# Two-layer convolution block on one core: the tail of layer 0 is rewritten so that its tiles keep pixels on partitions

## The chip, the cores and the metric

The kernel runs on one core of one Trainium2 chip. The metric is the device time of one execution in microseconds. A core has a matrix engine (TensorE, PE in the profile, its weight loads as PEld), a vector engine (VectorE, DVE), an activation engine (ScalarE, ACT), GpSimd (POOL) and SyncE (SP), which only issues DMAs here. Each engine runs its own instructions strictly in the order in which the program lists them; semaphores make one engine wait for another.

## The reference

The input `x` has shape (2, 256, 128, 128): two images of 256 channels. Two residual layers follow each other, each behind a group norm:

```python
x = x + L0(gn(x))          # three deformable branches, a 1x1 convolution and an MLP
x = x + conv3x3(gn(x), ternary(weight)) + bias
# L0, for xg = gn(x):
x_i = gelu(ln2d(deform_dw(xg, conv3x3(xg, off_w_i)), bw_i, bb_i))   # i = 1, 2, 3; dilations 1, 9, 12
c   = conv_w @ xg + conv_b                                          # 1x1
out = ln2d(x_1 + x_2 + x_3 + c, n1_w, n1_b)
h   = gelu(out @ mlp_w1.T + mlp_b1) @ mlp_w2.T + mlp_b2             # per pixel, 256 -> 512 -> 256
out = ln2d(h + out, n2_w, n2_b)
```

`ln2d` normalises each pixel over its 256 channels and then applies a weight and a bias per channel. The inputs set `bw_i`, `n1_w`, `n2_w` to ones and `bb_i`, `n1_b`, `n2_b` to zeros.

## The kernel before, in words

The program has three stages. Stage A normalises `x`, writes it pixel by pixel to a table in DRAM, computes the offsets of the three branches and from them bilinear weights ("hats"), which also go to DRAM. The middle stage samples the table, and runs the rest of layer 0 (the "tail") beside the sampling. Stage C is the second layer's convolution. A flag computed between stage A and the middle stage (`beyond`) chooses between the fast sampling (`sample_near`) and a general path (`sample_any`); the inputs here take the fast one.

**Sampling.** A unit is (image, block of two image rows, branch). For each unit the vector engine builds a matrix `A` by multiplying hats (`build`, L1088, three instructions for the three rows of taps), into one of two `A` buffers. Then come two passes, one for each half of the channels (`sample`). In a pass the matrix engine multiplies 11 tiles of the table by `A` into PSUM tiles `pm` (L1173; an fp32 matmul shows as two records, so 22 records a pass); ACT copies each pair of tiles from PSUM to a tile `ev` (L1182); the vector engine accumulates from `ev` into a ring of image rows, one `SCALAR_TENSOR_TENSOR` for each tap (`accumulate`, L1150). There are four `pm` banks and three `ev` tiles. `A` for unit u+2 is built by the vector engine ahead of the accumulation of the second pass of unit u: it can be built only when the matrix engine is done with unit u, and the matrix engine can't start unit u+2 before it is built.

**A cycle.** Four image rows (512 pixels, a "group") take two row blocks of three branches, so six units or twelve passes. These are called pass 0 to pass 11 below: 0 and 1 are the first branch of the even row block, 2 and 3 the second, 4 and 5 the third, 6 to 11 the same for the odd row block. There are 64 groups.

**The tail.** When the rows of a group are complete in a branch's ring, a generator `Tail.branch` is begun. It runs in steps beside the sampling: `sample` calls `tail.advance()` before and in the middle of each pass's matmuls, and each step issues its instructions there. A `yield n` lets n advances go by; a second number says how many big tiles the branch holds from then on, which `may` weighs against `VBUFS` (9 tiles) and `PEAK`. All instructions on PE, ACT and DVE in this stage are pinned to the order in which Python issues them (`pin`). For one branch of a group the tail does:

- `normalised`: eight 128x128 transposes on PE (L824) turn the ring's rows so that pixels lie on partitions, with a correction by bf16 matmuls (L832); two ACT copies bring them to a tile `T` (L840); four `bn_stats` and four `bn_aggr` on DVE give mean and variance of every pixel (L848, L850); four small POOL instructions give scale and bias (L852 to L855); after five advances, four ACT instructions normalise `T` in place (L859); eight more transposes (L871) turn it back to channels on partitions, into two PSUM tiles `zc`;
- two ACT instructions apply GELU with `bw` and `bb` from PSUM (L887); the result is added to the earlier branches' through DRAM (`g12d`; L901, L931);
- after the third branch, `finish` adds the 1x1 product of `x` minus its mean (L802 `pc`, L927 on DVE), normalises the sum (`normalised`, then L937), does both products of the MLP (L802 `hp` and `h`, GELU L950, sum L965), normalises again (`normalised`), applies `n2_w`, `n2_b` and `x` (L980, L986), takes statistics for layer 1 (L990) and stores.

So `normalised` runs five times for each group, with 16 transposes each time.

Of the kernel before, what the change touches and what calls it, by code (L numbers as in the profile page):

```python
# [19 lines left out]
P = 128  # L20
W = 128
C = 256
KC = C // P
HID = 512
MC = HID // P
R = 4
NG = R * W
# [7 lines left out]
LN_EPS = 1e-6  # L35
# [15 lines left out]
BRS = (0, 1, 2)  # L51
NORMS = 3
VBUFS = 9
PEAK = 3
GAP = 2
LAG = 5
XCLS = (0, 1, 3, 9, 11)
# [14 lines left out]
def conv_preact_kernel(ctx: ExitStack, tc: tile.TileContext, t: dict, out: bass.AP):  # L72
    nc = tc.nc
    x = t["x"]
    NB, _, H, _ = x.shape
# [13 lines left out]
    nc.vector.tensor_copy(ident_b, ident)  # L89
    mhalf = const.tile([P, NG // P], F32, name="mhalf")  # L90
    nc.vector.memset(mhalf, -0.5)

    later = []

# [5 lines left out]
    def load_now():  # L100
# [50 lines left out]
    x1d = dram("x1d", [C, HW])  # L151
# [306 lines left out]
    with ExitStack() as actx:  # L458
        psum = actx.enter_context(tc.tile_pool(name="ps_a", bufs=1, space=PSUM))

        def gps():
            return psum.tile([P, 512], F32, name="gnps", tag="tp", bufs=2)

        ap = actx.enter_context(tc.tile_pool(name="apool", bufs=1))
        dxs = sorted({d * s for d in DILS for s in (-1, 0, 1)})
        k = {
            "dxs": dxs,
            "zero": ap.tile([P, C], F32, name="zero"),
            "wz": ap.tile([P, KC, NZ], F32, name="wz"),
            "shift": ap.tile([P, len(dxs), P], F32, name="shift"),  # L470
            "mid": ap.tile([P, ZG, NOFF], F32, name="mid"),
            "hatw": ap.tile([P, 2, NTAP * NH], BF16, name="hatw"),
            "parts": [ap.tile([P, 2, ZG, P], BF16, name=f"parts{i}") for i in range(2)],
            "zr": ap.tile([P, ZRING, NZ], F32, name="zr"),
            "planes": [ap.tile([P, 2, NG], BF16, name=f"planes{i}") for i in range(2)],
        }
        nc.vector.memset(k["zero"], 0.0)
        for parts in k["parts"]:
            nc.vector.memset(parts, 0.0)
        XT = min(4, NGRP)  # L480
        beside = store_signs(ap)
        for b in range(NB):
            stats = ap.tile([P, KC, NGRP, 6], F32, name=f"stats1_{b}", tag=f"stats1_{b}")
            for c in range(KC):
                for g0 in range(0, NGRP, XT):
                    xt = ap.tile([P, XT * NG], F32, name="xt", tag="xt", bufs=3)
                    nc.sync.dma_start(
                        xt,
                        x[b, c * P : (c + 1) * P].rearrange("p h w -> p (h w)")[
                            :, g0 * NG : (g0 + XT) * NG  # L490
                        ],
                    )
                    for j in range(XT):
                        nc.vector.bn_stats(stats[:, c, g0 + j, :], xt[:, j * NG : (j + 1) * NG])
            if b == 0:
                load_now()
                nc.sync.dma_start(k["wz"], t["wz"].rearrange("(k p) n -> p k n", p=P))
                nc.sync.dma_start(k["shift"], t["shift"])
                nc.sync.dma_start(k["mid"], t["mid"])
                hatw = ap.tile([P, 2, NTAP * NH], F32, name="hatw32", tag="xt", bufs=3)  # L500
                nc.sync.dma_start(hatw, t["hatw"])
                nc.vector.tensor_copy(k["hatw"], hatw)
                pattern = ap.tile([P, NG], F32, name="pattern", tag="xt", bufs=3)
                nc.sync.dma_start(pattern[HALF : HALF + NPAT], t["pattern"])
# [12 lines left out]
            phase_a(b, ap, psum, k, beside)  # L517
        for _ in beside:
            pass
# [218 lines left out]
    with tc.tile_pool(name="mpool", bufs=1) as mpool:  # L738
        with tc.tile_pool(name="ps_m", bufs=1, space=PSUM) as ps_m:
            miss = missing(ps_m, mpool)  # L740
        ids = miss["ids"]
        farall = small.tile([P, 1], F32, name="farall", tag="farall")
        nc.gpsimd.partition_all_reduce(farall, miss["worst"], P, bass.bass_isa.ReduceOp.max)
        flag = const.tile([P, 1], I32, name="flag")
        nc.vector.tensor_scalar(flag, farall, 0.0, None, ALU.is_gt)
        beyond = nc.values_load(flag[0:1, 0:1], min_val=0, max_val=1)
# [6 lines left out]
    class Tail:  # L753
# [48 lines left out]
                    nc.tensor.matmul(out, lhsT=w, rhs=v, start=i == 0, stop=i == n - 1)  # L802
                )

        def normalised(self, z, src, what=None):

            pool, pin = self.pool, self.pin
            NB4 = NG // P  # L810
            while self.norms == NORMS:
                yield 1
            self.norms += 1
            T = self.tile("T")
            Tv = T.rearrange("p k n -> p (k n)").rearrange("p (j c) -> p j c", c=C)
            S = self.spots.get(what and what[0::2])
            tps = [self.bank("tp") for h in range(NB4 // 2)]
            for h in range(NB4 // 2):
# [19 lines left out]
            for h in range(NB4 // 2):  # L838
                pin(
                    nc.scalar.copy(  # L840
                        Tv[:, 2 * h : 2 * h + 2, :].rearrange("p j c -> p (j c)"), tps[h]
                    )
                )
            self.read.add(what)
            st = pool.tile([P, NB4, 6], F32, name="st", tag="st", bufs=NORMS)
            mv = pool.tile([P, NB4, 2], F32, name="mv", tag="mv", bufs=NORMS)
# [147 lines left out]
            )  # L994


    def sample_near(pool, psum, k):

        pin = tc.keep_in_program_order
        count = pool.tile([P, NG], F32, name="count")  # L1000
        nc.sync.dma_start(count, t["count"].partition_broadcast(P))
        tail = Tail(pool, psum, pin)
        units = [(b, Rt, br) for b in range(NB) for Rt in range(NR) for br in BRS]
        xts, hbs, owners, begun = {}, {}, {}, set()
        done = {(b, br): 0 for b in range(NB) for br in BRS}
# [618 lines left out]
```

## Time and profile before

| | |
|---|---|
| runs shown | 7072.38, 7077.51, 7089.49 us; median 7077.51 |
| the profiled execution | 7086.97 us; span of its instructions 7085.2 us |
| stage A | from the start to 975 us, when the first hats are loaded back |
| middle stage, first to last sampling matmul | 983.6 to 5896.0 us |
| rest of the tails, without sampling | 5896 to 6035 us |
| stage C | from 6046 us on |

The page lists for each engine its busy time; a view by windows gives the same for any stretch of the span; the view of groups gives, for each line and shape, count, busy time and mean duration. Records of matmuls overlap: a record of PE lasts some 0.16 us longer than the time until the next one starts. What an instruction costs its engine is therefore read from the start of one run of equal instructions to the start of what follows it, in the timeline. The timeline merges equal instructions (`x8`) and shows in brackets how long the engine sat idle before them and what ended that.

### The profile page before, as it was taken

To read this page: it belongs to the slowest core of one execution; us is meant where nothing else is said; L and a number is where in the kernel's file an instruction comes from. 1 tells how busy PE (TensorE), PEld (TensorE's weight loads), DVE (VectorE), ACT (ScalarE), POOL (GpSimd) and SP (SyncE) were. 2 spreads that over 40 slices of the span, in tenths; PEclk is the share of its full clock that TensorE was granted. 3 is DMA by queue.
4 is the path that set the end of the run, shared out by engine and by line. 5 is a ranking of instruction groups with operands and counts; after the bars stand their busy time and mean duration, and the time that the engine had idled before them with its cause. 6 is when DMAs were issued, how large, how long until landed. Compare 5 with 4: busy or idle time off the path is not lost. (4 is left out here: it accounts for less than half of the span.)

```text
span 7085.2 us, 104557 instructions
## 1 busy us (share of the span) xinstructions
PE 6716.0 (95%) x33906; PEld 5091.4 (72%) x33906; DVE 5861.9 (83%) x13016; ACT 4654.2 (66%) x9398; POOL 811.4 (11%) x1307
## 2 busy tenths in 40 slices
PE   6899969999999999999999999999999999899999
PEld 3455558888888888888788888888888885344444
DVE  7766658999989999998689899989989985875775
ACT  2344437788878878877777788788878876332332
POOL 0000010111111111111111111111111111000000
PEclk9999979999999999999999999999999999999999
DMA  8876657777777777776667777777777762221211
GB/s 289 254 205 185 189 152 219 221 215 210 213 213 213 217 212 217 211 209 202 179 195 219 208 218 213 213 213 213 216 208 216 217 203 86 100 81 69 75 70 51
DMA packets 671955, 1330.29 MB, mean 188 GB/s; under 512 B 109736, under 2 KB 290008, under 8 KB 667168
## 3 DMA queue, kind: packets, MB, share of 16 engines
q1 hardware_dynamic: 653408, 1288.49, 61.3%
q10 hardware_dynamic: 17408, 33.56, 1.5%
q8 instruction: 273, 4.47, 0.3%
q14 instruction: 290, 2.38, 0.1%
q0 software_dynamic: 576, 1.39, 0.1%
HBM read 1057.07 MB, written 266.08 MB: 187 GB/s over the span
## 5 line engine op out<-in xcount | busy, mean ns | idle before, releaser
L1173 PE MATMUL pm<-A,xs 96*128 96x216 f32 (+2 forms) x17424 | 3267.5, 342 | 132.3 <-ACT ev L1182 81.3
L1173 PEld LDWEIGHTS pm<-A,xs 96*128 96x128 f32 x17424 | 3055.0, 193 | 367.7 <-issue 152.8
L1150 DVE SCALAR_TENSOR_TENSOR ring<-ev,defw,ring 128x256 f32<-128x256 f32 (+4 forms) x6372 | 2482.9, 451 | 160.1 <-ACT ev L1182 100.3
L1182 ACT COPY ev<-pm 128x432 f32<-128x432 f32 (+2 forms) x4752 | 2032.5, 475 | 708.2 <-PE pm L1173 592.6
L1088 DVE TENSOR_TENSOR A<-hy,hx 96x768 f32<-96x768 f32 (+1 forms) x1124 | 1005.2, 943 | 287.1 <-PE pm L1173 235.8
L1458 PE MATMUL pc<-cring,signs 128*128 128x512 bf16 x4608 | 1007.6, 382 | 20.0 <-ACT cring L1405 13.3
L1458 PEld LDWEIGHTS <-signs 128*128 128x128 bf16 x4608 | 452.4, 98 | 574.5 <-issue 30.1
L859 ACT ACTIVATE T<-T,rs 128x256 f32<-128x256 f32 x1280 | 663.2, 592 | 20.8 <-POOL rs L855 20.7
L852 POOL TENSOR_SCALAR rs<-mv 128x4 f32<-128x4 f32 x320 | 123.2, 385 | 4205.2 <-DVE mv L850 2905.1
L802 PE MATMUL hp<-T,w 128*128 128x512 f32 x1024 | 482.9, 595 | 2.5 <-ACT T L937 2.5
L329 PE MATMUL pz<-wz,xa 128*128 128x486 f32 x1024 | 467.0, 585 | 16.7 <-DVE zr L336 16.7
L848 DVE BATCH_NORM_STATS2 st<-T 128x6 f32<-128x256 f32 x1280 | 446.7, 410 | 30.3 <-ACT T L840 30.3
L802 PE MATMUL h<-hT,w 128*128 128x512 f32 x1024 | 460.5, 592 | 0.0
L1132 ACT ACTIVATE ring<-ev,defw 128x256 f32<-128x256 f32 (+1 forms) x856 | 404.5, 485 | 24.1
L1466 ACT ACTIVATE o<-xl,l1b 128x1024 f32<-128x1024 f32 x64 | 73.5, 1148 | 500.9 <-DMA out_x<-o 427.3
L854 POOL TENSOR_TENSOR rs<-rs,mhalf 128x4 f32<-128x4 f32 x320 | 400.6, 1252 | 0.0
L840 ACT COPY T<-tp 128x512 f32<-128x512 f32 x640 | 344.1, 593 | 71.8 <-PE tp L832 53.1
L1405 ACT CAST cring<-D 128x2048 bf16<-128x2048 f32 (+1 forms) x140 | 245.0, 1755 | 185.8 <-PE pc L1458 127.4
L871 PE MATMUL zc<-ident,T 128*128 128x128 f32 x2560 | 342.2, 277 | 13.2 <-ACT T L859 9.5
L950 ACT ACTIVATE hT<-hp,b 128x512 f32<-128x512 f32 x256 | 176.0, 687 | 264.5 <-PE hp L802 262.9
L435 ACT ACTIVATE hb<-ph 96x512 f32<-96x512 f32 (+1 forms) x384 | 214.0, 593 | 183.8 <-PE ph L428 171.9
L871 PEld LDWEIGHTS zc<-ident,T 128*128 128x128 f32 x2560 | 303.4, 143 | 31.8 <-ACT T L859 12.8
(206 smaller groups left out, 5655.9 us busy)
## 6 DMA issues: line engine op xcount, KB each, us to landing
hy<-hats SPq DMA_DIRECT2D x1112, 288.0 KB
hx<-hats SPq DMA_DIRECT2D x1112, 288.0 KB
xs<-tables SPq DMA_DIRECT2D x1452, 96.0 KB
g12d<-T SPq DMA_DIRECT2D x128, 512.0 KB
other<-g12d SPq DMA_DIRECT2D x128, 512.0 KB
hats<-hb SPq DMA_DIRECT2D x64, 720.0 KB
hats<-hb SPq DMA_DIRECT2D x64, 576.0 KB
xl<-x1d SPq DMA_DIRECT2D x56, 640.0 KB
```

Source lines behind the costliest of these rows:

```text
L329: nc.tensor.matmul(pz[:, 0:NZ], lhsT=xt[:, c, r, :], rhs=k["wz"][:, c, :], start=c == 0, stop=c == KC - 1,)
L802: nc.tensor.matmul(out, lhsT=w, rhs=v, start=i == 0, stop=i == n - 1)
L848: pin(nc.vector.bn_stats(st[:, j, :], Tv[:, j, :]))
L854: nc.gpsimd.tensor_tensor(rs[:, 0, :], rs[:, 0, :], mhalf[:, 0:NB4], ALU.pow)
L859: nc.scalar.activation(Tv[:, j, :], Tv[:, j, :], AF.Identity, scale=rs[:, 0, j : j + 1], bias=rs[:, 1, j : j + 1],)
L871: nc.tensor.transpose(zc[:, j * P : (j + 1) * P], Tv[:, j, c * P : (c + 1) * P], ident)
L1088: nc.vector.tensor_tensor(dst, hy[:, i0:i1].rearrange("p i t w -> p t i w"), hx[:, i0:i1].rearrange("p i t w -> p t i w"), ALU.mult,)
L1132: pin(nc.scalar.mul(dst, src, w))
L1150: pin(nc.vector.scalar_tensor_tensor(dst, src, w, dst, ALU.mult, ALU.add))
L1173: nc.tensor.matmul(pm[:, j, 0:n], lhsT=xts[b, Rt][T + j][:, c * P : (c + 1) * P], rhs=A[:, m0:m1, AO + (T + j) * CI : AO + (T + j + 1) * C ...
L1182: nc.scalar.copy(ev[:, m0:m1, T * CI : (T + nt) * CI].rearrange("p m (t j) -> p t m j", j=CI), pm[:, 0:nt, 0:n].rearrange("p t (m j) -> p ...
L1458: nc.tensor.matmul(pc[:, bank, :], lhsT=w[:, m * P : (m + 1) * P], rhs=xc[:, i, k, t * JC : (t + 1) * JC, kx : kx + W], start=j == 0, stop ...
```

## The change

The tail of the fast path gets its own class, `PixelTail`, which keeps pixels on partitions all the way. `turned` is the first part of `normalised` (turn the ring's rows, copy them to a tile). Then:

- GELU is applied in place on that tile, with each pixel's scale and bias (four ACT instructions of 128x256 take the place of four normalising ones and of the two from PSUM); the way back to channels falls away for the three branches. `g12d` holds tiles as they lie.
- the 1x1 product is computed with pixels on partitions: the pixels of `x` are the stationary operand and the weights (256 columns) the moving one; the bias comes from a matmul with three rows of ones and the bias split in three bf16 parts (`ones3`, `row3`). The second product of the MLP is done in the same way.
- the two later norms need no turn any more; the first is turned to channels for the first product of the MLP (`channels`, two ACT copies to `S`), the second for the end.
- `bw`, `bb`, `n1_w`, `n1_b` aren't applied; where one of them isn't one or zero, the flag sends the program to the general path, whose tail (`Tail`) is as before. `conv_b` and `mlp_b2` come as a new input `rows`.
- `PEAK` is 4 in place of 3, and the numbers of the yields differ.

```diff
@@ -51,7 +51,7 @@
 BRS = (0, 1, 2)
 NORMS = 3
 VBUFS = 9
-PEAK = 3
+PEAK = 4
 GAP = 2
 LAG = 5
 XCLS = (0, 1, 3, 9, 11)
@@ -89,6 +89,27 @@
     nc.vector.tensor_copy(ident_b, ident)
     mhalf = const.tile([P, NG // P], F32, name="mhalf")
     nc.vector.memset(mhalf, -0.5)
+    ones3 = const.tile([3, P], BF16, name="ones3")
+    nc.vector.memset(ones3, 1.0)
+    row3 = const.tile([3, 2, C], BF16, name="row3")
+    convb3, b23 = row3[:, 0, :], row3[:, 1, :]
+    def split_rows(pool):
+        def tmp(name, dt=F32):
+            return pool.tile([3, 2, C], dt, name=name, tag="xt", bufs=3)
+        rows, part, sel = tmp("rows"), tmp("part", BF16), tmp("sel")
+        nc.sync.dma_start(rows, t["rows"].partition_broadcast(3))
+        nc.vector.memset(sel, 0.0)
+        for i in range(3):
+            nc.vector.tensor_copy(part, rows)
+            nc.vector.scalar_tensor_tensor(
+                sel, part, ident[0:3, i : i + 1], sel, ALU.mult, ALU.add
+            )
+            nc.vector.tensor_tensor(rows, rows, part, ALU.subtract)
+        nc.vector.tensor_copy(row3, sel)
 
     later = []
 
@@ -500,6 +521,7 @@
+                split_rows(ap)
@@ -739,6 +761,19 @@
         with tc.tile_pool(name="ps_m", bufs=1, space=PSUM) as ps_m:
             miss = missing(ps_m, mpool)
         ids = miss["ids"]
+        odd = small.tile([P, 8 * KC], F32, name="odd", tag="odd")
+        for i, (v, usual) in enumerate(((bw, 1.0), (bb, 0.0))):
+            nc.vector.tensor_scalar(
+                odd[:, 3 * KC * i : 3 * KC * (i + 1)], v.rearrange("p b k -> p (b k)"), usual,
+                None, ALU.not_equal,
+            )
+        for i, (v, usual) in enumerate(((n1w, 1.0), (n1b, 0.0))):
+            nc.vector.tensor_scalar(
+                odd[:, (6 + i) * KC : (7 + i) * KC], v, usual, None, ALU.not_equal
+            )
+        anyodd = small.tile([P, 1], F32, name="anyodd", tag="anyodd")
+        nc.vector.tensor_reduce(anyodd, odd, AX.X, ALU.max)
+        nc.vector.tensor_tensor(miss["worst"], miss["worst"], anyodd, ALU.max)
         farall = small.tile([P, 1], F32, name="farall", tag="farall")
         nc.gpsimd.partition_all_reduce(farall, miss["worst"], P, bass.bass_isa.ReduceOp.max)
         flag = const.tile([P, 1], I32, name="flag")
@@ -802,17 +837,10 @@
                     nc.tensor.matmul(out, lhsT=w, rhs=v, start=i == 0, stop=i == n - 1)
                 )
 
-        def normalised(self, z, src, what=None):
-            pool, pin = self.pool, self.pin
+        def turned(self, Tv, src, what):
+            pin = self.pin
             NB4 = NG // P
-            while self.norms == NORMS:
-                yield 1
-            self.norms += 1
-            T = self.tile("T")
-            Tv = T.rearrange("p k n -> p (k n)").rearrange("p (j c) -> p j c", c=C)
             S = self.spots.get(what and what[0::2])
             tps = [self.bank("tp") for h in range(NB4 // 2)]
             for h in range(NB4 // 2):
@@ -841,6 +869,19 @@
                         Tv[:, 2 * h : 2 * h + 2, :].rearrange("p j c -> p (j c)"), tps[h]
                     )
                 )
+        def normalised(self, z, src, what=None):
+            pool, pin = self.pool, self.pin
+            NB4 = NG // P
+            while self.norms == NORMS:
+                yield 1
+            self.norms += 1
+            T = self.tile("T")
+            Tv = T.rearrange("p k n -> p (k n)").rearrange("p (j c) -> p j c", c=C)
+            self.turned(Tv, src, what)
             self.read.add(what)
             st = pool.tile([P, NB4, 6], F32, name="st", tag="st", bufs=NORMS)
             mv = pool.tile([P, NB4, 2], F32, name="mv", tag="mv", bufs=NORMS)
@@ -994,12 +1035,186 @@
             )
 
 
+    class PixelTail(Tail):
+        def moments(self, rows):
+            pool, pin = self.pool, self.pin
+            n = len(rows)
...
+            return rs
+        def scaled(self, rows, rs, func):
+            for j, row in enumerate(rows):
+                self.pin(
+                    nc.scalar.activation(
+                        row, row, func, scale=rs[:, 0, j : j + 1], bias=rs[:, 1, j : j + 1]
+                    )
+                )
+        def entered(self):
+            while self.norms == NORMS:
+                yield 1
+            self.norms += 1
+        def product(self, name, S, bias, pairs):
+            for h in range(NG // P // 2):
+                bank = self.bank(name).rearrange("p (j c) -> p j c", c=C)
+                for j in range(2):
+                    px = slice((2 * h + j) * P, (2 * h + j + 1) * P)
+                    self.pin(
+                        nc.tensor.matmul(
+                            bank[:, j, :], lhsT=ones3, rhs=bias, start=True, stop=False
+                        )
+                    )
+                    for i, (v, w) in enumerate(pairs):
+                        self.pin(
+                            nc.tensor.matmul(
+                                bank[:, j, :], lhsT=v[:, px], rhs=w,
+                                start=False, stop=i == len(pairs) - 1,
+                            )
+                        )
+                Sh = S[:, 2 * h : 2 * h + 2, :]
+                self.pin(nc.vector.tensor_tensor(Sh, bank, Sh, ALU.add))
+                yield
+        def channels(self, rows, c):
+            zc = self.bank("zc")
+            for j, row in enumerate(rows):
+                self.pin(
+                    nc.tensor.transpose(
+                        zc[:, j * P : (j + 1) * P], row[:, c * P : (c + 1) * P], ident
+                    )
+                )
+            return zc
+        def branch(self, b, br, g, y):
+            pin = self.pin
+            gv = g12d[b].rearrange("c f -> (c f)").rearrange("(g p e) -> g p e", p=P, e=KC * NG)[g]
+            xv = x[b].rearrange("(k p) h w -> p k (h w)", p=P)[:, :, g * NG : (g + 1) * NG]
+            yield from self.entered()
+            v = self.tile("v")
+            vf = v.rearrange("p k n -> p (k n)")
+            vv = vf.rearrange("p (j c) -> p j c", c=C)
+            rows = [vv[:, j, :] for j in range(NG // P)]
+            self.turned(vv, y, (b, br, g))
+            self.read.add((b, br, g))
+            rs = self.moments(rows)
+            yield 5, min(1 + br, 2)
+            self.scaled(rows, rs, AF.Gelu)
+            self.norms -= 1
+            if br == 0:
+                yield 2
+                nc.sync.dma_start(gv, vf)
+                return
+            other = self.tile("other")
+            of = other.rearrange("p k n -> p (k n)")
+            nc.sync.dma_start(of, gv)
+            if br == 1:
+                yield 2
+                pin(nc.vector.tensor_tensor(vf, vf, of, ALU.add))
+                yield 2
+                nc.sync.dma_start(gv, vf)
+                return
+            yield 1, 3
+            xn = self.tile("xn")
+            nc.sync.dma_start(xn, xv)
+            yield 2
+            pin(nc.vector.tensor_tensor(vf, vf, of, ALU.add))
+            yield 2, 2
+            for c in range(KC):
+                pin(
+                    nc.scalar.activation(
+                        xn[:, c, :], xn[:, c, :], AF.Identity, bias=negmean[b][:, c : c + 1]
+                    )
+                )
+            yield 1
+            for _ in self.product(
+                "pc1", vv, convb3, [(xn[:, c, :], convs[b][:, c, :]) for c in range(KC)]
+            ):
+                pass
+            yield 3, 1
+            yield from self.entered()
+            rs = self.moments(rows)
+            yield 5
+            self.scaled(rows, rs, AF.Identity)
+            self.norms -= 1
+            yield 2, 2
+            S = self.tile("S")
+            for c in range(KC):
+                pin(nc.scalar.copy(S[:, c, :], self.channels(rows, c)))
+            yield 1, 3
+            hT = []
+            for m in range(MC):
+                if m % KC == 0:
+                    hT.append(self.tile("hT"))
+                hp = self.bank("hp")
+                self.matmul(hp, [(w1[:, c, m * P : (m + 1) * P], S[:, c, :]) for c in range(KC)])
+                pin(
+                    nc.scalar.activation(
+                        hT[-1][:, m % KC, :], hp, AF.Gelu, bias=b1[:, m : m + 1]
+                    )
+                )
+                yield 1, 4 if m < MC - 1 else 3
+            for n, _ in enumerate(
+                self.product(
+                    "h2", vv, b23,
+                    [(hT[m // KC][:, m % KC, :], w2[:, m, :]) for m in range(MC)],
+                )
+            ):
+                yield 1, 3 if n == 0 else 1
+            yield 2, 2
+            yield from self.entered()
+            rs = self.moments(rows)
+            xr = self.tile("xr")
+            nc.sync.dma_start(xr, xv)
+            yield 5
+            self.scaled(rows, rs, AF.Identity)
+            self.norms -= 1
+            for c in range(KC):
+                pin(
+                    nc.scalar.activation(
+                        xr[:, c, :], xr[:, c, :], AF.Identity, bias=n2b[:, c : c + 1]
+                    )
+                )
+            yield 2
+            for c in range(KC):
+                zc = self.channels(rows, c)
+                pin(
+                    nc.vector.scalar_tensor_tensor(
+                        xr[:, c, :], zc, n2w[:, c : c + 1], xr[:, c, :], ALU.mult, ALU.add
+                    )
+                )
+                pin(nc.vector.bn_stats(stats2[b][:, c, g, :], xr[:, c, :]))
+            yield 2, 1
+            nc.sync.dma_start(
+                x1d[b].rearrange("(k p) f -> p k f", p=P)[:, :, g * NG : (g + 1) * NG], xr
+            )
     def sample_near(pool, psum, k):
 
         pin = tc.keep_in_program_order
         count = pool.tile([P, NG], F32, name="count")
         nc.sync.dma_start(count, t["count"].partition_broadcast(P))
-        tail = Tail(pool, psum, pin)
+        tail = PixelTail(pool, psum, pin)
         units = [(b, Rt, br) for b in range(NB) for Rt in range(NR) for br in BRS]
         xts, hbs, owners, begun = {}, {}, {}, set()
         done = {(b, br): 0 for b in range(NB) for br in BRS}
@@ -1584,6 +1799,7 @@
         "mid": mid,
         "aux": aux,
         "misc": misc,
+        "rows": np.stack([l0["conv_b"], l0["mlp_b2"]]),
         "tapid": np.tile(np.arange(1, NTAP + 1, dtype=np.float32), (P, 1)),
         "count": np.arange(NG, dtype=np.float32),
         "defw": np.stack([l0[f"def_w{i}"].reshape(C, 9) for i in (1, 2, 3)], 1).reshape(C, NTAP),
```

More of the change, by code (lines that the diff above doesn't have):

```diff
@@ L994, in finish @@
             )
+    class PixelTail(Tail):
+        def moments(self, rows):
+            pool, pin = self.pool, self.pin
+            n = len(rows)
+            st = pool.tile([P, n, 6], F32, name="st", tag="st", bufs=NORMS)
+            mv = pool.tile([P, n, 2], F32, name="mv", tag="mv", bufs=NORMS)
+            for j in range(n):
+                pin(nc.vector.bn_stats(st[:, j, :], rows[j]))
+            for j in range(n):
+                pin(nc.vector.bn_aggr(mv[:, j, :], st[:, j, :]))
+            rs = pool.tile([P, 2, n], F32, name="rs", tag="rs", bufs=NORMS)
+            nc.gpsimd.tensor_scalar(rs[:, 0, :], mv[:, :, 1], LN_EPS, None, ALU.add)
+            nc.gpsimd.tensor_scalar(rs[:, 1, :], mv[:, :, 0], -1.0, None, ALU.mult)
+            nc.gpsimd.tensor_tensor(rs[:, 0, :], rs[:, 0, :], mhalf[:, 0:n], ALU.pow)
+            nc.gpsimd.tensor_tensor(rs[:, 1, :], rs[:, 1, :], rs[:, 0, :], ALU.mult)
+            return rs
[141 more added lines that the diff above has]
+            )
```

## Prediction

> **What bounds the kernel now.** I read the page first, then the windows, the groups, and the timeline of single engines.
>
> ```profile
> span 7085.2 us, 104557 instructions
> PE 6716.0 (95%) x33906; PEld 5091.4 (72%) x33906; DVE 5861.9 (83%) x13016; ACT 4654.2 (66%) x9398; POOL 811.4 (11%) x1307
> ```
>
> The change touches the middle stage, 983.6 to 5896.0 us. There a window of 1200 us says which engine is full:
>
> ```profile
> 1600.00:2800.00 1200.00, 1182.96 (x6147) 1010.07 (x6146) 1102.73 (x2665) 970.92 (x2041) 191.77 (x308) 1.00 0.73 213
> ```
>
> The columns are PE, PEld, DVE, ACT, POOL, clock, DMA share, GB/s. PE is busy 98.6% of the time, DVE 91.9%, ACT 81%. So PE is the bound, but DVE is close: the question is what a relief of PE alone is worth. The timeline of DVE through one cycle of twelve passes answers it (left out are the rows between, which show no idle time):
>
> ```profile
> 2189.20 3.13 DVE L1150 SCALAR_TENSOR_TENSOR ring<-ev,defw,ring 128x256 f32<-128x256 f32 x8 [1.38 <-ACT ev L1182]
> 2192.25 0.75 DVE L965 SCALAR_TENSOR_TENSOR T<-h,b,T 128x512 f32<-128x512 f32 x1
> 2197.10 2.69 DVE L1088 TENSOR_TENSOR A<-hy,hx 96x768 f32<-96x768 f32 x3 [4.11 <-PE pm L1173]
> 2199.72 3.12 DVE L1150 SCALAR_TENSOR_TENSOR ring<-ev,defw,ring 128x256 f32<-128x256 f32 x8
> 2202.76 1.39 DVE L848 BATCH_NORM_STATS2 st<-T 128x6 f32<-128x256 f32 x4
> 2204.07 0.36 DVE L850 BATCH_NORM_AGGREGATE mv<-st 128x2 f32<-128x6 f32 x4
> 2204.35 3.61 DVE L1150 SCALAR_TENSOR_TENSOR ring<-ev,defw,ring 128x256 f32<-128x256 f32 x8
> ...
> 2235.45 2.69 DVE L1088 TENSOR_TENSOR A<-hy,hx 96x768 f32<-96x768 f32 x3
> 2238.05 6.67 DVE L1150 SCALAR_TENSOR_TENSOR ring<-ev,defw,ring 128x256 f32<-128x256 f32 x16
> ```
>
> DVE waits once a cycle, 4.11 us, at the build of `A` in pass 11, until PE ends that pass; this build starts at 1887.30, 1964.29, 2041.88, 2119.00, 2197.10 and 2274.09, so cycles last 77.0 to 78.1 us, 77.36 on average. Between waits DVE works back to back and falls behind: the build at 2235.45 belongs to pass 5, whose matmuls PE had ended five microseconds before. Now PE:
>
> ```profile
> 2198.21 4.91 PE L1173 MATMUL pm<-A,xs 96*128 96x216 f32 x26
> 2203.55 1.73 PE L1173 MATMUL pm<-A,xs 96*128 96x216 f32 x8 [0.42 <-ACT ev L1182]
> ...
> 2206.86 4.18 PE L1173 MATMUL pm<-A,xs 96*128 96x216 f32 x22
> 2210.88 3.60 PE L802 MATMUL pc<-xn,convw 128*128 128x512 f32 x8
> 2214.32 4.18 PE L1173 MATMUL pm<-A,xs 96*128 96x216 f32 x22
> 2218.34 1.04 PE L871 MATMUL zc<-ident,T 128*128 128x128 f32 x8
> 2219.21 4.18 PE L1173 MATMUL pm<-A,xs 96*128 96x216 f32 x22
> ...
> 2241.45 0.60 PE L832 MATMUL tp<-extra,S 128*128 128x256 bf16 x4
> 2241.89 2.36 PE L1173 MATMUL pm<-A,xs 96*128 96x216 f32 x12
> ```
>
> Start to start: a `pm` record 4.02/22 = 0.183 us, a record of 512 fp32 columns 0.43, a transpose 0.87/8 = 0.109, a bf16 matmul of 256 columns 0.44/4 = 0.11. A cycle has 264 `pm` (48.2), 16 `hp` and 16 `h` (13.8), 8 `pc` (3.4), 80 transposes (8.7) and 12 corrections (1.3): 75.4 us. The other 1.6 to 2.7 us are waits, for `ev` in passes 1 and 7 and for the ring.
>
> **The change on PE.** The order in which the built program's instructions stand shows 40 transposes less for each group (24 turns back and 16 turns of the two later norms): 40 x 0.109 = -4.36 us. The products cover the same columns in records of 256, which I take as 0.217, half of 0.43 with a little on top (+0.1 in all; lower end 0, upper end 0.02 for each of 48, 1 us). Eight matmuls with ones are new; the nearest row is the correction, also bf16 and 256 columns: 8 x 0.11 = +0.88 (lower end 0.109 for the fewest columns seen, so the same; upper end 0.217, that of an fp32 record). Sum -3.4 us a cycle, to 72.0.
>
> [...] But transposes start 0.109 apart while the record of each load lasts 0.143, so loads overlap here and columns set the pace.
>
> **The change on ACT.** Away go L887 (six a group, 279.0/384 = 0.73), and four copies L840 (344.1/640 = 0.54); L859 stays twenty (0.52 each), twelve of them now GELU, whose price I take as the same, since L887 (0.73, GELU) and L937 (91.7/128 = 0.72, no GELU) agree; L937 becomes copies (-0.18 each). Sum 6 x 0.73 + 4 x 0.54 + 2 x 0.18 = -6.9 us of some 62 a cycle. ACT was not the bound, so this is worth nothing by itself; without it PE's waits for `ev` would grow.
>
> **The change on DVE.** The same kinds in the same number: 20 `bn_stats`, two sums from PSUM for each product (taken as 0.72 like L927; the lower end is 0.63 like L1438, which has no PSUM operand, 0.4 us a cycle less; upper end 0.75). So DVE keeps its 71 us (1102.73/1200 x 77.36).
>
> **Where they meet.** The order of tail work among the passes is new, and here the gain is lost. On DVE, nothing changes but places: between the builds of passes 9 and 3 now stand six accumulations (two of each branch), four norms' statistics, the sums of `pc`, both sums with `other`, the final step and three more builds. Before, between the builds of passes 11 and 5, stood the same with three norms' statistics, and took 2238.05 - 2197.10 = 40.95 us without a gap. So the new stretch takes 40.95 + 1.59 (2202.76 to 2204.35) = 42.5 us. PE can't start pass 6 before the build of pass 3 is done; and DVE's build in pass 9 waits for PE's pass 9, because the heavy steps now stand in passes 6 to 9: pass 6 4.02 + 0.87 + 1.72, pass 7 4.02 + 3.44 + 1.31, pass 8 4.02 + 1.72 + 0.22 + 3.47, pass 9 to its last `pm` 4.02 + 0.22 + 3.47; together 32.5. The loop is 42.5 + 32.5, plus two handovers of 0.2 (as PE's 2196.90 to DVE's 2197.10), plus a wait of `hp` in pass 6 for the copies to `S`, which stand on ACT behind three `ev` copies that wait for DVE's pass 3: 0 to 0.9, I take 0.4. That is 75.8 us for cycles that now take 77.0. The longer cycles have more accumulations (0.5 us on average over six) in the same stretch: 76.3 on average, against 77.36: -1.1 us. PE alone (72.0 and a microsecond or two of waits for ACT) would be shorter by 2 to 3 us: PE waits that long at the start of pass 6. Before, the same loop had slack: the build of pass 5 ended at 2238.1 and PE began pass 8 at 2241.9.
>
> **SP and POOL.** The stores and loads of `g12d` have the same size; POOL the same instructions. `other`, `xr` and `xn` (512 KB each) now stand together on SP ahead of the hats that the build of pass 1 needs; DMA is 73% busy and that build comes 13 us after the one before, as it did, so I take 0; if hats come late it lies on the loop.
>
> **Sum.** 47 full cycles at -1.1: -52. Some seven at the images' edges, where `pm` has fewer columns: -7. Five at the seam of the images, where PE alone bounds: -2 each, -10 (0 to -17). The first four cycles, without all tails: -4. The tails after the last pass take 138 us, of which PE is busy 113; there 128 transposes fall away and 32 matmuls with ones come, -128 x 0.109 + 32 x 0.11 = -10.4; as a fifth of that stretch isn't PE's, I take -8. Stage A: splitting the bias rows adds 11 DVE instructions of 0.4 to 0.74 us and the test of the norms' weights six of 0.15, 7 us, where DVE has gaps of 4.14, 0.85, 2.60 and 1.35: +3 (0 to +7). Together -78: from 7086.97 to 7009. The median of the runs is 9.5 below the profiled execution, so 7077.5 - 78 = 7000.
>
> **Rivals.** (1) PE stays the bound: DVE's stretch is shorter than I sum it (cheaper sums, fewer gaps). For it: PE is at 98.6%. Against it: that stretch has no idle row. A cycle of 72.0 + 1.5 gives 47 x 3.9 = -183 and the same -26 besides: 6870. (2) Slower: DVE's stretch gains a wait, at the build of pass 1 for hats behind those three loads, or for GELU behind `other`. All of it counts, since DVE has no slack there; from 1.1 us a cycle it decides, 3 us give 47 x 1.9 = +89 - 26: 7140. For it: builds did wait for `hx` 50.9 us in the run; against it: 0.4 of that fell in the window above. (3) The two cancel: 0.9 for `S`, the upper ends on PE, 1 us of gaps: 7060 to 7095.
>
> **How the numbers follow.** A change under 0.3% (21 us) can't be told from none. Forecast as worked out, 6950 to 7055: 0.50. Between it and rival 1, or rival 1: 0.24. Cancelled: 0.12. Rival 2: 0.14. Faster 0.74, same 0.12, slower 0.14. The range leaves out rival 1 at its full size (about 0.1) and a wait of over 2 us a cycle (under 0.1): 6900 to 7095; the forecast's own range is 6950 to 7055.
>
> **What would show it.** Right: in the same window PE near 95%, DVE 93% or more, ACT near 72%; a new wait of PE's `pm` for DVE's build of `A`, 2 to 3 us a cycle, at the start of pass 6; DVE's one long wait at the build of pass 9; cycles of 75.8 to 77.1 us. Wrong: no such wait and cycles of 74 (rival 1), or DVE idle between the builds of passes 9 and 3 (rival 2). The matmuls with ones starting over 0.2 apart would prove their price wrong, GELU over 0.6 us that of ACT.

## The result, and the profile after

The changed kernel takes 7452.15 us (median of 4 runs, 7417.39 to 7496.26) against 7080.02 us before (4 runs): a ratio of 1.0521, 95% interval 1.0491 to 1.0552. It is 5% slower; I had forecast 1.1% faster. The profiled execution took 7496.26 us and is the longest of the four. The page's first lines, and the window of the middle stage in which PE was busy 98.6% before (columns: PE, PEld, DVE, ACT, POOL, clock, DMA share, GB/s):

```profile
span 7494.4 us, 102700 instructions
PE 6864.0 (92%) x33394; PEld 5270.3 (70%) x33394; DVE 5867.1 (78%) x13034; ACT 4313.2 (58%) x8758; POOL 1069.6 (14%) x1307
...
1600.00:2800.00 1200.00, 1131.36 (x5553) 976.38 (x5552) 1018.61 (x2471) 824.96 (x1746) 251.15 (x292) 0.95 0.71 198
```

No engine is full any more: PE 94%, DVE 85%, ACT 69%. Two columns moved that the prediction had not touched: the clock fell from 1.00 to 0.95, and POOL works 251 us in place of 192 though it does the same instructions for fewer groups. Nearly all of the loss lies in the middle stage: it lasts 5313.9 us (996.4 to 6310.3) in place of 4912.4. What follows is 5 us shorter. Stage A ends 12.8 us later, but in the variants below, which share it, it ends anywhere from 979 to 995 us.

One cycle (2036.78 to 2119.02, 82.24 us, the usual length; passes 0 to 5, pass 6, passes 7 to 11) shows where the clock goes:

```profile
2036.78:2069.06 32.28, 30.74 (x162) 27.72 (x161) 31.61 (x76) 26.67 (x58) 13.77 (x11) 1.00 0.86 250
2069.06:2080.61 11.55, 9.60 (x35) 7.95 (x36) 9.52 (x22) 8.03 (x17) 0.35 (x1) 0.70 0.99 249
2080.61:2119.02 38.41, 37.99 (x195) 32.11 (x194) 30.64 (x86) 22.87 (x48) 4.01 (x8) 1.00 0.53 145
```

Pass 6 holds 22 sampling records, eight transposes and half of the first MLP product, 6.6 us of work, and takes 11.55. The timeline of the four engines around its start:

```profile
2063.58 1.40 DVE L1050 BATCH_NORM_STATS2 st<-v 128x6 f32<-128x256 f32 x4
2064.89 0.36 DVE L1052 BATCH_NORM_AGGREGATE mv<-st 128x2 f32<-128x6 f32 x4
2065.17 1.19 DVE L1132 TENSOR_TENSOR v<-v,other 128x1024 f32<-128x1024 f32 x1
2066.28 2.68 DVE L1303 TENSOR_TENSOR A<-hy,hx 96x768 f32<-96x768 f32 x3
...
2065.41 1.04 POOL L1054 TENSOR_SCALAR rs<-mv 128x4 f32<-128x4 f32 x1 [15.36 <-DVE mv L1052]
2066.53 0.78 POOL L1055 TENSOR_SCALAR rs<-mv 128x4 f32<-128x4 f32 x1
2067.28 1.71 POOL L1056 TENSOR_TENSOR rs<-rs,mhalf 128x4 f32<-128x4 f32 x1
2069.07 0.35 POOL L1057 TENSOR_TENSOR rs<-rs 128x4 f32<-128x4 f32 x1
...
2066.44 0.52 ACT L1397 COPY ev<-pm 128x432 f32<-128x432 f32 x1 [0.21 <-PE pm L1388]
2069.45 2.08 ACT L1064 ACTIVATE v<-v,rs 128x256 f32<-128x256 f32 x4 [2.50 <-POOL rs L1057]
2071.43 1.14 ACT L1397 COPY ev<-pm 128x432 f32<-128x432 f32 x3
...
2069.06 0.97 PE L1388 MATMUL pm<-A,xs 96*128 96x216 f32 x4 [0.84 <-issue]
2071.98 3.25 PE L1388 MATMUL pm<-A,xs 96*128 96x216 f32 x8 [1.95 <-ACT ev L1397]
2075.02 1.91 PE L1101 MATMUL zc<-ident,v 128*128 128x128 f32 x8
```

Read from the top. DVE ends the moments of the norm behind the 1x1 product. POOL makes scale and bias of them, and needs 4.0 us for its four small steps, which take 1.8 to 2.2 us in most norms of the kernel before. ACT has come to the scaling (L1064) and stands for 2.50 us; three copies from PSUM are behind it. PE has filled its four `pm` banks and stands, 0.84 us for `A` (the profile names no releaser; the build ends 0.1 us before) and 1.95 for a bank. Then comes a second cost, nearly as large: the eight records after that wait take 3.04 us (2071.98 to 2075.02) in place of 1.46, the transposes 0.214 us each in place of 0.109. PE runs at half clock: the clock's records give it a share of 0.5 from 2070.57 to 2077.40.

In the next cycle PE stands at the same place for about as long (0.58 and 1.95 us), and the clock stays at 1.00:

```profile
2153.90 1.73 PE L1388 MATMUL pm<-A,xs 96*128 96x216 f32 x8 [1.95 <-ACT ev L1397]
2155.46 1.04 PE L1101 MATMUL zc<-ident,v 128*128 128x128 f32 x8
```

There the eight records take 1.56 us, and pass 6 takes 8.90 (2150.98 to 2159.88) in place of 11.55. So half clock cost 2.65 us here, on top of the wait.

For a number over the whole stage I add up, from the clock's records in the trace, half of every spell at half clock ("clock lost" below). Before, the middle stage lost 55 us in 14 spells, none in the full cycles; after, 298 in 88. So by this count 243 of the 401 us that the stage grew are the clock's. That is an upper bound: the spell above counts as 3.4 us and cost 2.65.

### The profile page after: what moved, and what is told of

Same layout as the page of the kernel before. It is cut to its first block, busy times and chain, and to the rows that moved or that the text cites. A ratio compares the mean times of both kernels' runs of the same rounds, so it can differ in the third digit from the quotient of the medians.

```text
span 7494.4 us, 102700 instructions
## 1 busy us (share of the span) xinstructions
PE 6864.0 (92%) x33394; PEld 5270.3 (70%) x33394; DVE 5867.1 (78%) x13034; ACT 4313.2 (58%) x8758; POOL 1069.6 (14%) x1307
## 5 line engine op out<-in xcount | busy, mean ns | idle before, releaser
L1388 PE MATMUL pm<-A,xs 96*128 96x216 f32 (+2 forms) x17424 | 3359.0, 350 | 363.2 <-ACT ev L1397 241.9
L1388 PEld LDWEIGHTS pm<-A,xs 96*128 96x128 f32 x17424 | 3146.6, 198 | 557.8 <-ACT ev L1397 305.7
L1054 POOL TENSOR_SCALAR rs<-mv 128x4 f32<-128x4 f32 x320 | 202.3, 632 | 4344.5 <-DVE mv L1052 3741.1
L1064 ACT ACTIVATE v<-v,rs 128x256 f32<-128x256 f32 x1280 | 664.4, 593 | 225.4 <-POOL rs L1057 225.4
L1087 PE MATMUL h<-w,hT 128*128 128x256 f32 x2048 | 511.1, 392 | 1.2 <-ACT hT L1171 1.2
L837 PE MATMUL hp<-S,w 128*128 128x512 f32 x1024 | 485.3, 598 | 0.1
L1050 DVE BATCH_NORM_STATS2 st<-v 128x6 f32<-128x256 f32 x1280 | 446.8, 410 | 14.1 <-ACT v L868 14.0
L1087 PEld LDWEIGHTS h<-w,hT 128*128 128x128 f32 x2048 | 367.7, 189 | 72.5 <-ACT hT L1171 2.2
L1093 DVE TENSOR_TENSOR v<-h,v 128x512 f32<-128x512 f32 x128 | 88.4, 690 | 420.5 <-PE h L1087 410.1
L1087 PE MATMUL pc<-convw,xn 128*128 128x256 f32 x1024 | 348.6, 467 | 47.3 <-ACT xn L1144 46.7
```

What stands on the lines that cost most here:

```text
L1050: pin(nc.vector.bn_stats(st[:, j, :], rows[j]))
L1064: nc.scalar.activation(row, row, func, scale=rs[:, 0, j : j + 1], bias=rs[:, 1, j : j + 1])
L1087: nc.tensor.matmul(bank[:, j, :], lhsT=v[:, px], rhs=w, start=False, stop=i == len(pairs) - 1,)
L1388: nc.tensor.matmul(pm[:, j, 0:n], lhsT=xts[b, Rt][T + j][:, c * P : (c + 1) * P], rhs=A[:, m0:m1, AO + (T + j) * CI : AO + (T + j + 1) * C ...
```

## The experiments

A cycle is taken as the mean of 48 full ones of each run's profiled execution (cycles 5 to 28 and 38 to 61); ratios are to the kernel before, in the same sessions.

| run | us | ratio, 95% interval | cycle | clock lost |
|---|---|---|---|---|
| before | 7080 to 7091 | 1 | 77.44 | 55 |
| changed | 7452.15 | 1.0521, 1.0491 to 1.0552 | 83.73 | 298 |
| e1_later | 7137.48 | 1.0066, 1.0049 to 1.0083 | 77.59 | 100 |
| e2_const | 7190.76 | 1.0143, 1.0120 to 1.0166 | 79.20 | 134 |
| e3_rows | 7343.35 | 1.0359, 1.0327 to 1.0390 | 81.13 | 261 |
| e4_fill | 7321.27 | 1.0316, 1.0289 to 1.0344 | 81.09 | 121 |
| e7_xn | 7404.32 | 1.0446, 1.0427 to 1.0466 | 82.17 | 267 |
| e5_best | 7539.13 | 1.0639, 1.0625 to 1.0654 | 85.53 | 379 |
| e6_rows_later | 7072.20 | 0.9980, 0.9970 to 0.9991 | 76.66 | 130 |
| e8_act | 7014.78 | 0.9901, 0.9883 to 0.9919 | 75.47 | 105 |
| e9_act4 | 7045.63 | 0.9949, 0.9929 to 0.9969 | 76.56 | 124 |

**The product half a pass later** (in `PixelTail.branch`, ahead of the subtraction of the mean):

```diff
             pin(nc.vector.tensor_tensor(vf, vf, of, ALU.add))
-            yield 2, 2
+            yield 3, 2
```

> Edit: the 1x1 product and all that follows it in the tail come one advance (half a pass) later; no work is added or removed. Theory H (held): the scaling behind the 1x1 product stands on ACT ahead of copies from PSUM, and waits there 2.2 us for POOL, whose input DVE delivers late; PE runs out of PSUM banks at pass 6, stands idle for more than half of a 3.4 us stretch, and is then given half clock, which lengthens the loop between DVE and PE. H expects that half a pass is enough for ACT to find its scale ready: middle stage at clock 0.99 or more, cycles of 76.5 to 77.5 us in place of 83.7, total 7050 to 7130. Rival P (price): the eight matmuls with ones cost 0.41 us each in place of 0.11, and PE's own work is what the cycle lasts for: the same work, so 7400 to 7490. Rival D (loads): other, xn and xr stand ahead of hats on SP: xn gets no more time, 7380 to 7490.

One number in the order of issue brings back 315 us of the 372 (7452.15 to 7137.48). The window shows the clock at 1.00 and ACT's wait for POOL at 0.8 us, where it was 41.7 (the changed kernel's row stands last):

```profile
1600.00:2800.00 1200.00, 1169.41 (x6002) 1013.83 (x6002) 1096.15 (x2659) 877.89 (x1875) 254.80 (x308) 1.00 0.76 213
...
ACT v L1064 <- POOL rs L1057: 0.8, 3, 0.3
...
ACT v L1064 <- POOL rs L1057: 41.7, 14, 10.7
```

The mean cycle, 77.59, is slightly over the expected 76.5 to 77.5, and the total 7 us over its range. Of the 100 us of clock that it still loses hardly any lie in the full cycles; they lie in the first cycles and at the images' edges. The expectation was wrong on one point: here `xn` does get half a pass more before ACT reads it, so this run alone does not rule out the loads.

**That one norm without its wait for POOL**:

```diff
             yield 5
-            self.scaled(rows, rs, AF.Identity)
+            self.scaled(rows, unit, AF.Identity)
```

> Edit: the scaling behind the 1x1 product takes its scale and bias from a constant tile (1 and 0), so it waits for nothing on POOL; the moments are still computed, but this one norm is left out of the result. H expects ACT's waits for POOL (41.7 us in the window 1600 to 2800) to be nearly gone and PE's for ev to fall from 47.8 to under 20 there; cycles of 77 to 79.5 us, total 7100 to 7250. P and D expect no change: 7400 to 7490.

This kernel leaves the norm out of its result: its four scaling instructions take a scale of 1 and a bias of 0 that are always ready. The work, its order and the loads are as they were; only the dependence on POOL is gone, and with it 261 us (in the range). What is left over the kernel before has other names in the window: PE's 1x1 product waits 15.6 us for `xn`, DVE's builds 14.8 for `hx`.

**The load of `xn` one advance earlier**:

```diff
-            yield 1, 3
             xn = self.tile("xn")
             nc.sync.dma_start(xn, xv)
+            yield 1, 3
             yield 2
```

(and the branch holds a third tile from its first wait on).

> Edit: of the changed kernel only the load of xn is issued one advance earlier, together with other. Theory D: the cycles that are longer than the usual 82.2 us (mean 83.7) come from xn landing late, on which the 1x1 product waits (9.8 us in the window 1600 to 2800) and after which the clock drops; and part of the whole is D's: mean cycle 82.2 or less, total 7330 to 7390. H alone: the usual cycle stays at 82 and ACT's waits for POOL at 40 us in the window, whatever xn does: 7390 to 7470.

Both had a part right. The median cycle stays at 81.9 and ACT still waits 33.7 us for POOL, near the 40 that H gave; but the mean falls from 83.73 to 82.17, as D said. Most of the cycles of 85 to 95 us had been those in which `xn` landed late: in 13 of these 16 ACT had waited over 0.7 us for it (in 10 of the other 32 too), and with the earlier load it never does. The total, 7404, lies in H's range and not in D's. This is a smaller cause beside the first, 48 us or 0.6%.

**More work on PE, where it stands**:

```diff
+                if T < 4 and br == 0 and c == 0 and Rt % 2:
+                    if T == 0:
+                        warm = tail.bank("warm")
+                    for i in range(8 if T == 0 else 14):
+                        pin(
+                            nc.tensor.matmul(
+                                warm[:, 0:C], lhsT=ident_b, rhs=tail.extra[:, 0, :],
+                                start=True, stop=True,
+                            )
+                        )
                 pm = psum.tile([P, 2, 256], F32, name="pm", tag="pm", bufs=4)
```

> Edit: 22 bf16 matmuls of 256 columns, 2.4 us, are added on PE once a cycle, where it stands idle: eight ahead of the first matmul of pass 6 and fourteen ahead of the third; nobody reads what they write. H expects that they fill the idle time and keep the clock: clock lost in the middle stage (302 us in all) under 120 us, most cycles at 79 to 80 us, total 7250 to 7350, faster with more work. P expects the added work in full, 64 x 2.4 = 154: 7600. D expects at least no gain: 7430 to 7600.

22 matmuls a cycle whose product nobody reads make the kernel 131 us faster, and the lost clock falls from 298 to 121 us (H gave under 120). The same place in the timeline of PE:

```profile
2108.12 1.04 PE L1389 MATMUL warm<-extra,ident_b 128*128 128x256 bf16 x8
2108.99 0.90 PE L1398 MATMUL pm<-A,xs 96*128 96x216 f32 x4
2109.72 1.69 PE L1389 MATMUL warm<-extra,ident_b 128*128 128x256 bf16 x14
2111.78 1.73 PE L1398 MATMUL pm<-A,xs 96*128 96x216 f32 x8 [0.37 <-ACT ev L1407]
2113.35 1.04 PE L1101 MATMUL zc<-ident,v 128*128 128x128 f32 x8
```

ACT still waits 44.8 us for POOL in the window, but the eight records take 1.57 us and a transpose 0.109 again. So the wait and the price of the clock on top of it are two things: with ACT's wait left as it was, 131 us came back.

**The ones over 128 rows** (three of ones, the rest zero, for `ones3`; the bias in three rows, the rest zero, for `row3`):

```diff
-    ones3 = const.tile([3, P], BF16, name="ones3")
-    row3 = const.tile([3, 2, C], BF16, name="row3")
+    ones3 = const.tile([P, P], BF16, name="ones3")
+    row3 = const.tile([P, 2, C], BF16, name="row3")
```

> Edit: the matmuls with ones take 128 rows in place of 3 (125 of them zero); the sum is the same. If their price comes from the few rows, one starts 0.11 us before the next in place of 0.21, and the records around it lose their extra 0.1 us: 2.4 us less PE work a cycle. H expects that PE then merely waits longer at pass 6, except for the 1.2 us of passes 8 and 9, which lie on the loop: cycles 1 to 1.5 us shorter, total 7350 to 7400. P expects all 2.4 us in 64 cycles: 7300. If the price does not come from the rows: no change, 7420 to 7490.

The timeline of PE in the changed kernel, then in this one:

```profile
2178.66 2.36 PE L1388 MATMUL pm<-A,xs 96*128 96x216 f32 x12
2180.95 0.28 PE L1081 MATMUL h<-row,ones 3*128 3x256 bf16 x1
2181.16 1.99 PE L1087 MATMUL h<-w,hT 128*128 128x256 f32 x8
2183.08 0.28 PE L1081 MATMUL h<-row,ones 3*128 3x256 bf16 x1
```

```profile
2158.66 2.35 PE L1390 MATMUL pm<-A,xs 96*128 96x216 f32 x12
2160.85 0.28 PE L1083 MATMUL h<-row,ones 128*128 128x256 bf16 x1
2160.96 1.89 PE L1089 MATMUL h<-w,hT 128*128 128x256 f32 x8
2162.69 0.27 PE L1083 MATMUL h<-row,ones 128*128 128x256 bf16 x1
```

From one block to the next it is 2.13 us in the first and 1.84 in the second. Start to start, a matmul of three rows costs 0.208, the record before it 0.1 more than its usual 0.216 and the one behind it 0.1 more; with 128 rows it costs 0.109 and its neighbours nothing. 0.3 us each, 2.4 a cycle; the cycle gets 2.6 shorter, against the 1 to 1.5 that H gave it and nearer to P's 2.4. Part of the 2.6 is the clock, of which 37 us less are lost, 0.6 a cycle. The total, 7343, lies between P's 7300 and H's 7350 to 7400.

**Both, and a larger PEAK**. Two kernels with the later product and the ones over 128 rows; the first also has PEAK 5 in place of 4.

> Edit: the 1x1 product one advance later and the ones over 128 rows, as in the two runs before, and PEAK 5 in place of 4. With PE never idle for long (77.5 us a cycle at full clock with the product later) and 2.4 us less work on it, what H says is left is the loop of DVE and PE, in which passes 8 and 9 get 1.2 us shorter, and PE's need of 72: cycles of 74 to 76 us, against 77.4 of the kernel before, so 48 x 2 less and as much in proportion in the shorter cycles: total 6930 to 7040. Against it: if the later product only trades one wait for another that DVE sets (the cycle with it, 77.5, is 5 us over PE's need), the ones bring nothing: 7100 to 7140.

> Edit: the same with PEAK left at 4. If PEAK plays no part, as that of the fifth kernel within 0.5%; if it keeps steps of two groups apart that PEAK 5 lets overlap, 20 to 60 us slower than that one, at cycles of 74.5 to 76.5 us.

The second is 0.2% faster than the kernel before; the first, from which I expected the most, is the slowest of all. Its timeline (DVE, POOL, ACT, PE):

```profile
2155.79 0.36 DVE L1054 BATCH_NORM_AGGREGATE mv<-st 128x2 f32<-128x6 f32 x4
2156.07 2.66 DVE L1305 TENSOR_TENSOR A<-hy,hx 96x768 f32<-96x768 f32 x3
2158.65 3.16 DVE L1367 SCALAR_TENSOR_TENSOR ring<-ev,defw,ring 128x256 f32<-128x256 f32 x8
2161.73 1.22 DVE L1134 TENSOR_TENSOR v<-v,other 128x1024 f32<-128x1024 f32 x1
2162.87 3.12 DVE L1367 SCALAR_TENSOR_TENSOR ring<-ev,defw,ring 128x256 f32<-128x256 f32 x8
2165.91 2.69 DVE L1305 TENSOR_TENSOR A<-hy,hx 96x768 f32<-96x768 f32 x3
...
2157.91 1.71 POOL L1058 TENSOR_TENSOR rs<-rs,mhalf 128x4 f32<-128x4 f32 x1
2159.70 8.95 POOL L1059 TENSOR_TENSOR rs<-rs 128x4 f32<-128x4 f32 x1
...
2168.69 2.07 ACT L1066 ACTIVATE v<-v,rs 128x256 f32<-128x256 f32 x4 [9.48 <-POOL rs L1059]
...
2171.22 2.53 PE L1390 MATMUL pm<-A,xs 96*128 96x216 f32 x6 [9.23 <-ACT ev L1399]
```

A product of four numbers a partition takes 8.95 us: it ends 0.05 us after the second build (2165.91 to 2168.60), and DVE has no gap on the way. In the traces PEAK 5 puts the second branch's steps half a pass later: its turn on PE, and on DVE its sum with `other`, which with 4 stands ahead of the build (2150.83 and 2151.93 in e6_rows_later) and with 5 behind it. To tell whether that step alone holds the kernel up (L) or the order itself (K), the last two runs take that one step off POOL (`whole=False` leaves it out of the moments):

```diff
-            rs = self.moments(rows)
+            rs = self.moments(rows, whole=False)
             yield 5
+            for j in range(len(rows)):
+                pin(
+                    nc.scalar.activation(
+                        rs[:, 1, j : j + 1], rs[:, 1, j : j + 1], AF.Identity,
+                        scale=rs[:, 0, j : j + 1],
+                    )
+                )
             self.scaled(rows, rs, AF.Identity)
```

> Edit: the kernel with PEAK 5, the later product and the ones over 128 rows, but POOL's fourth step for the norm behind the 1x1 product (the product of negative mean and scale, 128x4) is done by ACT, in four instructions of 128x1 right ahead of the scaling. Theory L (lock): that step alone held up the kernel with PEAK 5: it took 8.95 us on POOL, from 2159.70 on, while DVE ran accumulations, a sum and a build without a gap, where it takes 0.2 us otherwise; ACT waited 9.48 us for it and PE 9.23. Without it the chain on POOL is 3.3 us (0.77 + 0.78 + 1.71), ACT's waits for POOL fall from 137.9 us in the window 1600 to 2800 to under 25, cycles from 85.5 to 74.5 to 76.5: total 6960 to 7060. Rival K: the order that PEAK 5 makes is itself at fault (DVE too late for the scaling in any case): ACT waits for POOL's third step nearly as long, 7400 to 7550.

> Edit: the same step moved to ACT in the kernel with PEAK 4, the later product and the ones over 128 rows. There POOL's fourth step took 0.23 us, so L expects 0.2 us less of ACT's 1.42 us wait and four small ACT instructions more: within 0.5% of 7072, 7040 to 7100. If the move itself is what helps or hurts (the ACT instructions cost over 0.5 us each, or POOL's other steps get slower), the difference shows here alone: 7100 or more.

L holds: with PEAK 5 the kernel goes from 7539.13 to 7014.78, and is 1.0% faster than the kernel before and 5.9% faster than the changed one. The clock in the window is 1.00 again:

```profile
1600.00:2800.00 1200.00, 1163.06 (x6175) 1042.81 (x6176) 1121.98 (x2730) 910.84 (x1995) 253.24 (x302) 1.00 0.79 220
...
ACT rs L1162 <- POOL rs L1058: 12.0, 16, 1.3
```

So the move is worth 524 us with PEAK 5. With PEAK 4, where that step took 0.23 us on POOL, it is worth 27 us, 0.4%, as L gave it room for.

## Why the prediction was wrong, point by point

- *PE's removed transposes and split products*: right. Transposes start 0.109 us apart, products of 256 columns 0.216.
- *The ones, 8 x 0.11 = 0.88 us, upper end 0.217 each*: mis-sized. They cost 0.41 each with what they add to their neighbours, 3.3 us a cycle, beyond my upper end. The nearest row had the same type and columns, but 128 rows. Why three rows cost more was not shown, only that with 128 rows (e3_rows) one costs 0.109 and its neighbours nothing extra.
- *DVE's work unchanged, its stretch from the build in pass 9 to that in pass 3 42.5 us*: right. It takes 42.9 (2107.87 to 2150.80), with DVE at 71.1 us a cycle in both kernels.
- *PE's passes 6 to 9, 32.5 us*: 36.2 (2150.98 to 2187.15) in a cycle without loss of clock. 1.2 more are the ones in passes 8 and 9; 2.3 are pass 6, 8.9 us in place of 6.6. I had put a wait of 0 to 0.9 there, for the copies to `S`. The wait that came is one step earlier, at the scaling itself.
- *"POOL the same instructions"*, costed at nothing: this is the step that failed first. The instructions are the same, but their place beside DVE's is new, and the four took 3.47 us on average in the window (2.52 before), 4.0 where it mattered. What stood behind the waiting ACT instruction (copies from PSUM, and so PE) I had not followed. No run separates POOL's slowness from DVE's late delivery of the moments; an estimate from these rows is that at 1.8 to 2.2 us for the four, some 2 of ACT's 2.50 us would not have come.
- *PE waits 2 to 3 us a cycle at the start of pass 6, for the build of `A`*: a wait of this length came at this place (0.84 + 1.95), but that is in part luck. Only the 0.84 is for the build; the 1.95 is for ACT's copies, which stood behind the scaling that waited for POOL. I counted the wait as time that PE had to spare. At 2.8 us it also brought half clock in most cycles, 3.7 us a cycle by the count above. The sum had no term for that, though the profile of before could have shown one: in the window from 1600 to 2800, where no wait of PE was over 0.6 us, the clock was 1.00; from 1000 to 1600, while the first tails set in and PE waited up to 6.0 us at a time, it was 0.95.
- *SP's three loads ahead of the hats, costed at 0*: 0.6% by the run with `xn` earlier; builds also waited 12.1 us for `hx` in the window.
- *The signature*: PE 95%, DVE 93% and ACT 72% were forecast, 94, 85 and 69 came. DVE's share is what tells it: the loop of DVE and PE was right as a form, and its PE half was too short.
- *Rivals*: slower had a chance of 0.14, by a wait of DVE's for hats or `other`. The sign was right, the place wrong: the wait that decided was ACT's for POOL.

The loop without the clock gives 79.3 us (the cycle from 2119.02; 42.9 + 36.2 and a handover of 0.2), against 75.8 to 77.1 forecast and already longer than the 77.36 before the change; the clock and late loads make 83.7 of it. With the waits mended the part of the forecast that holds is seen: the last variant but one, e8_act, is at 75.5 us and 7015, close to the 7000 that I gave the change as it stood. That it comes so close is partly chance: that kernel also has the product and the second branch's steps at other places, its ones over 128 rows and one step less on POOL.

## What to carry to other kernels

PE, which was no longer full, paid twice for a wait here: standing for 1.95 us cost those and, in the cycle shown, 2.65 us by half clock behind them. Filling the room that the change had made on PE brought back 131 us (e4_fill), so that is worth a trial where a change makes such room. Follow each small step on POOL to who waits for it, and look at what DVE does in that moment; the same four instructions took 1.8 us in the quickest norms of the kernel before and 12.3 in the cycle of e5_best shown above (2156.31 to 2168.65). And where an order is written out by hand, one place in it can be worth more than the work removed: 315 us here, where the removed work was forecast at 78.

## What the runs showed of the hardware

- In the traces of the kernel before and the changed one the clock's records know two shares, 1.0 and 0.5, and all but their first begin on a grid of 3.41 us. In the middle stage of the changed kernel all 76 stretches of this grid at full clock in which PE was busy for less than half were followed by one at half clock, and none of 1251 that were busy over 70%; between half and 70% it was 11 of 55 (each record is counted 0.165 us short, for the overlap). In the kernel before it was 12 of 15 under half, 1 of 8 between half and 70%, and none of 1382 over 70%. Half clock lasted one to three stretches in 82 of the 87 spells that began in the changed kernel's stage. The two cycles shown above differ in how their wait of 1.95 us lies to the grid: in the first PE was busy for 0.496 of the stretch that ended at 2070.57, and half clock followed; in the cycle from 2119.02 the border of two stretches, at 2152.49, lay inside the wait, PE was busy for 0.57 and 0.58 of them, and the clock stayed full. Why the clock is granted in this way was not shown.
- POOL's fourth small step (128x4, L1059) took 0.20 to 0.39 us in three norms of e5_best between 2100 and 2150, 3.26 in a fourth, and 8.95 in the norm shown above, while DVE ran accumulations, a sum and a build without a gap (some eighteen instructions); it ended 0.05 us after that build. In the changed kernel POOL's first step, begun at 2065.41 during the sum with `other`, took 1.04 us and ended 0.09 us after that sum. That POOL waits for DVE in these rows is what their times suggest; no run shows why, nor why a step gets in between two builds at one time and not at another.
- A bf16 matmul of 3 rows and 256 columns among fp32 ones cost 0.41 us with what it added to its neighbours (changed kernel), one of 128 rows 0.109 (e3_rows).
